# Decoder layer on one core: attention scores as two 64-column tiles in one run, root batches re-cut, mixing after the next queries' transposes

## The chip, the cores and the metric

One core of a Trainium2 chip runs the whole program in one launch. The time is device time in microseconds (us) for one execution. The engines are named as the profile names them: PE (matrix products; PEld is its weight load), DVE (VectorE), ACT (ScalarE), POOL (GpSimd) and SP (the queue that issues most transfers). All data is 32-bit floating point; each matrix product of the kernel appears in the trace as two matmul instructions.

## The reference

A pre-norm decoder layer over `x` of shape (16, 64, 512), in three residual steps:

```python
x = x + self_attention_over_batch(layernorm(x))
x = x + cross_attention(layernorm(x), ctx, mask, Wq, Wk, Wv, Wo, q_norm_w, k_norm_w)
x = x + mixture_of_experts(layernorm(x), gate_w, bias, Wg, Wu, Wd, Sg, Su, Sd)
```

The change lies in the cross attention. Each of the 16 batches has 64 query rows and 64 context rows, 32 query heads of 128, and 8 key/value heads, each shared by a group of 4 query heads:

```python
q = rmsnorm(q, q_norm_w)              # q = hidden @ Wq.T, root over the 128 of one head
k = rmsnorm(repeat(k, 4), k_norm_w)
scores = einsum('bhqd,bhkd->bhqk', q, k) / sqrt(128) + attention_mask
probs = softmax(scores)
out = einsum('bhqk,bhkd->bhqd', probs, v) ... @ Wo.T
```

The experts (16, the best 4 per token, plus a shared one) come after it and are not touched.

## The kernel before, in words

**Stages.** The 1024 tokens are 8 tiles of 128 rows; a tile holds two batches of 64. The batch attention, the keys and the values come first (to about 160 us), then the cross attention (about 165 to 745 us), then routing and experts. At 32-bit width the products with Wq and Wo are done by a seven-product scheme (`seven`, line 240) whose 14 matrix products are all recorded at line 254, with sums of the weights formed on POOL (`right_sums`, lines 235 to 238) and sums of the left operands (`left_sums`, lines 228 to 231).

**Steps of the cross attention.** `cross` (line 591) walks over pairs (g, u): g is one of 8 key/value heads, u one of 4 pairs of token tiles. For g from 0 to 5 a step does the following, in the text of the program:

- `softmaxed(g, u)` (line 490): for each of the two tiles, `normed_queries` (line 477) multiplies the raw queries by their roots on DVE (line 479), turns them on PE (line 482), and scales them by `q_norm_w` on the way out of PSUM on ACT (line 484) into `qt`. Then four products per tile form the scores (line 499). One product takes 128 columns of `qt` (two heads of 64 queries) as the stationary operand and 64 key columns as the moving one. DVE adds the mask (line 504), takes the maximum, subtracts it, ACT takes the exponential, DVE sums and normalises (lines 511 to 523).
- `queries(...)` (line 446): the Wq product for the step three places ahead, combined by DVE out of PSUM (lines 458 to 462), and the sums of squares on ACT (line 466).
- `projected(...)` (line 553): the Wo product of the step before, added into the running sums by DVE (lines 560 to 567).
- `attended(g, u, pr)` (line 526): turns the probabilities on PE (line 529), copies them out on ACT (line 533), mixes the values on PE (line 539), copies the result out on ACT (line 545) and forms the left sums on POOL (on DVE for g of 6 and 7).

For g of 6 and 7 the two heads alternate, and the steps also carry the layer norm, the routing and the table entries of the finished tiles.

**Roots.** `inverse_root` (line 440) takes a square root on ACT (line 442, each with a table load) and a reciprocal on DVE (line 443), for several tile pairs at once, whenever u is in `done`: after u = 0 and after u = 3 in every group but the last, so the second batch covers three tile pairs (24 roots per partition).

**Order.** The program's text is not the order on the engines: a scheduler places the instructions of each engine in a fixed order when the program is built, and semaphores enforce the data dependences. Each engine then works strictly through its own list. PSUM is used through rotating banks: 3 for the large products (`mm`), 2 for transposes (`tr`), 3 for scores, mixing and one of the seven products (`sc`).

In a regular step PE's list before the change is: probabilities turned, queries of the first tile turned, one Wq product, values mixed, scores of the first tile, queries of the second tile turned, two Wq products, scores of the second tile, the rest of Wq, all of Wo.

Of the kernel before, what the change touches and what calls it, by code (L numbers as in the profile page):

```python
# [25 lines left out]
AF = mybir.ActivationFunctionType  # L26
ALU = mybir.AluOpType
AX = mybir.AxisListType

P = 128  # L30
N, C, L = 16, 64, 512
NT = N * C // P
DC = L // P
KVH, GRP, HD = 8, 4, 128
# [8 lines left out]
SURE = 32  # L43
WB = 4
ROUND = float(3 << 22)


@with_exitstack
def decoder_layer(
# [25 lines left out]
    V, S, T, G = nc.vector, nc.scalar, nc.tensor, nc.gpsimd  # L75
# [17 lines left out]
    def tr_bank():  # L93
        return bank("tr", 2)

    def sc_bank():
        return bank("sc", 3)
# [6 lines left out]
    kT = [p.tile([P, KVH // 2, NT * P], F32, tag="kT", name="kT") for p in (kvp0, kvp)]  # L104
# [75 lines left out]
    qw_sb = const.tile([P, 1], F32, tag="qw", name="qw_sb")  # L180
# [52 lines left out]
    def right_sums(engine, t, w):  # L233
        b11, b12, b21, b22 = (w[:, 2 * k : 2 * k + 2, 256 * n : 256 * n + 256] for k in range(2) for n in range(2))
        engine.tensor_sub(t[:, 0], b12, b11)
        engine.tensor_sub(t[:, 1], b22, t[:, 0])  # L236
        engine.tensor_sub(t[:, 2], b21, t[:, 1])  # L237
        engine.tensor_sub(b12, b22, b12)
# [164 lines left out]
    for n0 in range(0, N, 4):  # L403
        for k in range(2):
            tp = tr_bank()
# [23 lines left out]
    q_raw, q_ss, q_rs = {}, {}, {}  # L429
# [16 lines left out]
    def queries(g, u):  # L446
        w = wq_tiles[g]
        if u == 0:
            q_ss[g] = small.tile([P, NT, GRP], F32, tag="qss", name="qss", bufs=2)
            if g > 0:  # L450
                right_sums(G, wq_t, w)
        raws = [work.tile([P, GRP, HD], F32, tag="qraw", name="qraw", bufs=8) for _ in range(2)]
        c1, c2 = (raw.rearrange("p (a h) d -> p a (h d)", a=2) for raw in raws)
        x, p7, p, r = seven(*xn_quarters(u), xn_sums[u], wq_t, w, sums_last=(g, u) == (0, 0))
        su = work.tile([P, 2, 256], F32, tag="su", name="su", bufs=1)
        u3 = work.tile([P, 256], F32, tag="u3", name="u3", bufs=1)
        S.copy(su[:, 0], x[:, 0])
        V.tensor_add(su[:, 1], x[:, 1], su[:, 0])
        V.tensor_add(u3, p7, su[:, 1])
        V.tensor_add(c1, p, su)  # L460
        V.tensor_add(c2, r, u3.unsqueeze(1).to_broadcast([P, 2, 256]))
        V.tensor_add(c1[:, 1], r[:, 1], c1[:, 1])
        for j, raw in enumerate(raws):
            for h in range(GRP):
                square = work.tile([P, HD], F32, tag="square", name="square", bufs=1)
                S.activation(square, raw[:, h, :], AF.Square, accum_out=q_ss[g][:, 2 * u + j, h : h + 1])  # L466
            q_raw[g, 2 * u + j] = raw

        done = (0, 1, 2, 3) if g == KVH - 1 else (0, 3)
        if u in done:  # L470
            first = max([k + 1 for k in done if k < u], default=0)
            span = 2 * (u + 1 - first)
            rs = inverse_root(q_ss[g][:, 2 * first : 2 * u + 2, :], [P, span, GRP], 1.0 / HD)
            for k in range(first, u + 1):
                q_rs[g, k] = rs[:, 2 * (k - first) : 2 * (k - first) + 2, :]

    def normed_queries(g, i):
        raw = q_raw.pop((g, i))
        V.tensor_mul(raw, raw, q_rs[g, i // 2][:, i % 2, :].unsqueeze(2).to_broadcast([P, GRP, HD]))  # L479
        tp = tr_bank()  # L480
        for j in range(GRP):
            T.transpose(tp[:, j * P : (j + 1) * P], raw[:, j, :], ident)  # L482
        qt = work.tile([P, 2, GRP, C], F32, tag="qt", name="qt", bufs=2)
        S.activation(  # L484
            qt.rearrange("p b h q -> p h b q"),
            tp.rearrange("p (h b q) -> p h b q", h=GRP, b=2), AF.Copy, scale=qw_sb,
        )
        return qt

    def softmaxed(g, u):  # L490
        sp = sc_bank()
        for j in range(2):
            i = 2 * u + j
            qt = normed_queries(g, i)
            for hp in range(2):
                for b in range(2):
                    k0 = i * P + b * C
                    at = ((j * 2 + hp) * 2 + b) * C
                    T.matmul(  # L499
                        sp[:, at : at + C], qt[:, b, 2 * hp : 2 * hp + 2, :],  # L500
                        kT[g // 4][:, g % 4, k0 : k0 + C], start=True, stop=True,
                    )
        pr = work.tile([P, 8, C], F32, tag="prob", name="prob")
        V.scalar_tensor_tensor(  # L504
            pr, sp.rearrange("p (a k) -> p a k", a=8), HD**-0.5,
            mask_sb.unsqueeze(1).to_broadcast([P, 8, C]), ALU.mult, ALU.add,
        )
        mx = small.tile([P, 8], F32, tag="mx", name="mx")
        sm = small.tile([P, 8], F32, tag="sm", name="sm")
        if g < KVH - 2:  # L510
            V.tensor_reduce(mx, pr, AX.X, ALU.max)
            V.tensor_sub(pr, pr, mx.unsqueeze(2).to_broadcast([P, 8, C]))
            S.activation(pr, pr, AF.Exp)
            V.tensor_reduce(sm, pr, AX.X, ALU.add)
        else:

            V.tensor_reduce(mx, pr, AX.X, ALU.max, negate=True)
            for a in range(8):
                S.activation(
                    pr[:, a, :], pr[:, a, :], AF.Exp, bias=mx[:, a : a + 1], accum_out=sm[:, a : a + 1]  # L520
                )
        V.reciprocal(sm, sm)
        V.tensor_mul(pr, pr, sm.unsqueeze(2).to_broadcast([P, 8, C]))
        return pr

    def attended(g, u, pr):
        tp = tr_bank()
        for a in range(4):
            T.transpose(
                tp[:, a * P : (a + 1) * P], pr[:, 2 * a : 2 * a + 2, :], ident  # L530
            )
        pt = work.tile([P, 2, 2 * P], F32, tag="pt", name="pt", bufs=1)
        S.copy(pt.rearrange("p j t -> p (j t)"), tp)
        at = work.tile([P, 2 * GRP, P], F32, tag="at", name="at", bufs=1)
        pv = [sc_bank() for _ in range(2)]
        for j in range(2):
            for b in range(2):
                rows = slice(b * C, (b + 1) * C)
                T.matmul(
                    pv[b][:, j * 256 : (j + 1) * 256],  # L540
                    v[g // 4][rows, 2 * u + j, g % 4 * HD : (g % 4 + 1) * HD], pt[rows, j, :],
                    start=True, stop=True,
                )
        for b in range(2):
            S.copy(at[:, :, b * C : (b + 1) * C], pv[b].rearrange("p (a q) -> p a q", a=2 * GRP))  # L545
        quarters = [at[:, 2 * k : 2 * k + 2, :] for k in range(4)]
        s = work.tile([P, 3, 2, P], F32, tag="sat", name="sat", bufs=1)
        left_sums(G if g < KVH - 2 else V, s, *quarters)
        return quarters, s
# [39 lines left out]
    late = []  # L589

    def cross(steps):
        for g, u in steps:
            if u == 1 and g + 2 < KVH:
                load_wq(g + 2)
            if u == 0 and g + 1 < KVH:
                load_wo(g + 1)
            pr = softmaxed(g, u)
            if g < KVH - 2:
                queries(*divmod(NT // 2 * g + u + 3, NT // 2))
            elif g == KVH - 2:  # L600
                queries(g + 1, u)
            if (g, u) == (KVH - 3, NT // 2 - 1):
                queries(g + 1, u)
            if late:
                projected(*late.pop())
            if (g, u) == (KVH - 1, NT // 2 - 1):
                shared_hidden(0, 0, mm_bank)
            late.append((g, u, *attended(g, u, pr)))
            if g == KVH - 2 and u > 0:
                summed(u - 1)  # L610
                normed_pair(u - 1)
                if u > 1:
                    entered(u - 2, 1)
            if g == KVH - 1 and u > 0:
                routed_pair(u - 1)
                entered(u - 1, 0)
            if (g, u) == (KVH - 2, 0):
                load_shared(0)
            if (g, u) == (KVH - 2, NT // 2 - 1):
                load_shared(1)  # L620
# [80 lines left out]
    def routed_pair(u):  # L701
# [64 lines left out]
        V.tensor_scalar(col, got, 1.0 / P, (P - 1) / (2.0 * P), ALU.mult, ALU.subtract)  # L766
        V.tensor_scalar(col, col, ROUND, ROUND, ALU.add, ALU.subtract)
        row = route.tile([P, 2 * TOPK], F32, tag="row", name="row", bufs=1)
# [335 lines left out]
```

## Time and profile before

| what | value |
|---|---|
| median of 3 runs | 1022.65 us (1020.56 to 1023.68) |
| profiled execution, its own time | 1023.92 us |
| its span, first to last instruction | 1022.1 us |
| mean granted clock of PE | 0.989 |
| PE busy | 975.9 us, 95% of the span |
| DVE, ACT, POOL busy | 527.0, 461.3, 329.1 us |
| scores on PE (line 499) | 512 matmuls, 69.7 us busy, 280 ns each |
| scaling of the turned queries on ACT (line 484) | 64 of 689 ns |
| roots times raw queries on DVE (line 479) | 64 of 1028 ns on average |

Busy time is the sum of the durations; matmuls overlap in the array, so the mean of 280 ns is longer than the distance from one matmul to the next. What a run of matmuls costs is read from the start times of a timeline. An average over the span hides the stages: PE is bound by its own work in the cross attention up to about 590 us, has waits between about 600 and 745 us, and works for the experts after that.

### The profile page before, as it was taken

To read this page: it belongs to the slowest core of one execution; us is meant where nothing else is said; L and a number is where in the kernel's file an instruction comes from. 1 tells how busy PE (TensorE), PEld (TensorE's weight loads), DVE (VectorE), ACT (ScalarE), POOL (GpSimd) and SP (SyncE) were. 2 spreads that over 40 slices of the span, in tenths; PEclk is the share of its full clock that TensorE was granted. 3 is DMA by queue.
4 is the path that set the end of the run, shared out by engine and by line. 5 is a ranking of instruction groups with operands and counts; after the bars stand their busy time and mean duration, and the time that the engine had idled before them with its cause. 6 is when DMAs were issued, how large, how long until landed. Compare 5 with 4: busy or idle time off the path is not lost. (4 is left out here: it accounts for less than half of the span.)

```text
span 1022.1 us, 13777 instructions
## 1 busy us (share of the span) xinstructions
PE 975.9 (95%) x4568; PEld 683.7 (67%) x4568; DVE 527.0 (52%) x1116; ACT 461.3 (45%) x1283; POOL 329.1 (32%) x356
## 2 busy tenths in 40 slices
PE   8999998999999999998999999979999999999994
PEld 3456555788888888887888887767664454544542
DVE  4565757674845756648457567667476111111110
ACT  2366662664454545545545475555530222222221
POOL 2132111421612516236235142032133444454433
PEclk9999999999999999999999999989899999999998
DMA  9120014200201102012010010000023966655663
GB/s 240 61 93 21 11 42 114 83 1 1 83 1 43 42 1 83 1 52 83 1 46 39 9 75 1 21 22 22 21 53 126 390 155 154 144 97 138 179 182 76
DMA packets 28956, 76.80 MB, mean 75 GB/s; under 512 B 4625, under 2 KB 9025, under 8 KB 26833
## 3 DMA queue, kind: packets, MB, share of 16 engines
q1 hardware_dynamic: 18160, 52.96, 15.4%
q0 software_dynamic: 10432, 22.66, 10.9%
q8 instruction: 38, 0.62, 0.2%
q14 instruction: 38, 0.30, 0.1%
q10 hardware_dynamic: 288, 0.26, 0.1%
HBM read 102.31 MB, written 14.97 MB: 115 GB/s over the span
## 5 line engine op out<-in xcount | busy, mean ns | idle before, releaser
L967 PE MATMUL sc<-w,xt 128*128 128x512 f32 x288 | 130.3, 593 | 2.3 <-DMA w<-in_wu_dram 2.2
L466 ACT ACTIVATE square<-qraw 128x128 f32<-128x128 f32 x256 | 79.1, 309 | 60.0 <-DVE qraw L460 29.2
L967 PEld LDWEIGHTS sc<-w,xt 128*128 128x128 f32 x288 | 51.8, 190 | 54.1 <-issue 52.2
L228 POOL TENSOR_TENSOR sat<-at 128x256 f32<-128x256 f32 x24 | 19.7, 821 | 210.0 <-ACT at L545 209.9
L972 DVE TENSOR_TENSOR z<-sc,z 128x256 f32<-128x256 f32 x36 | 15.3, 424 | 124.5 <-ACT z L971 120.0
L499 PEld LDWEIGHTS sc<-kT,qt 128*128 128x128 f32 x512 | 61.8, 191 | 19.1 <-ACT qt L484 11.0
L254 PE MATMUL mm<-wq_t,xns 128*128 128x256 f32 x256 | 70.7, 385 | 2.9 <-POOL wq_t L236 1.8
L254 PE MATMUL mm<-wo_sb,at 128*128 128x256 f32 x256 | 68.6, 394 | 5.0 <-ACT at L545 5.0
L254 PE MATMUL mm<-wq_sb,xnT 128*128 128x256 f32 x256 | 70.4, 381 | 0.0
L995 POOL DMA_INDIRECT out_dram<-y,idx x36 | 57.3, 1592 | 40.0 <-DMA out_dram<-y,idx 35.4
L499 PE MATMUL sc<-kT,qt 128*128 128x64 f32 x512 | 69.7, 280 | 0.3
L987 PE MATMUL mm<-w,zt 128*128 128x512 f32 x144 | 68.0, 594 | 1.6 <-DVE zt L980 1.0
L254 PE MATMUL mm<-wo_t,sat 128*128 128x256 f32 x256 | 67.5, 384 | 0.5 <-DVE sat L229 0.5
L479 DVE TENSOR_TENSOR qraw<-qraw,rs 128x512 f32<-128x512 f32 x64 | 63.5, 1028 | 0.5
L949 POOL DMA_INDIRECT xg<-rows_d,idx x40 | 39.6, 990 | 72.2 <-PE tr L978 49.5
L793 POOL DMA_INDIRECT table_d<-entry_sb,at_slot x24 | 25.6, 1068 | 114.7 <-DVE at_slot L760 108.3
L971 ACT ACTIVATE z<-sc 128x256 f32<-128x256 f32 x36 | 13.8, 383 | 107.0 <-PE sc L967 98.3
L504 DVE SCALAR_TENSOR_TENSOR prob<-sc,mask_sb 128x512 f32<-128x512 f32 x32 | 22.0, 688 | 77.2 <-PE sc L499 77.2
L254 PEld LDWEIGHTS mm<-wo_sb,at 128*128 128x128 f32 x256 | 49.6, 196 | 13.6 <-ACT at L545 6.8
L254 PEld LDWEIGHTS mm<-wo_t,sat 128*128 128x128 f32 x256 | 48.5, 193 | 7.1 <-POOL wo_t L237 0.6
L254 PEld LDWEIGHTS mm<-wq_t,xns 128*128 128x128 f32 x256 | 46.7, 190 | 8.7 <-POOL wq_t L236 2.0
L484 ACT ACTIVATE qt<-tr,qw_sb 128x512 f32<-128x512 f32 x64 | 43.8, 689 | 18.3 <-PE tr L482 18.3
(283 smaller groups left out, 2056.7 us busy)
## 6 DMA issues: line engine op xcount, KB each, us to landing
w<-in_wg_dram SPq DMA_DIRECT2D x40, 512.0 KB
w<-in_wu_dram SPq DMA_DIRECT2D x40, 512.0 KB
w<-in_wd_dram SPq DMA_DIRECT2D x40, 512.0 KB
wq_sb<-in_wq_dram SPq DMA_DIRECT2D x8, 1024.0 KB
wo_sb<-in_wo_dram SPq DMA_DIRECT2D x8, 1024.0 KB
xs<-in_x_dram SPq DMA_DIRECT2D x8, 256.0 KB
wv_sb<-in_wv_dram SPq DMA_DIRECT2D x2, 1024.0 KB
ct<-in_ctxt_dram SPq DMA_DIRECT2D x8, 256.0 KB
```

The source lines that it names most:

```text
L228: engine.tensor_add(s[:, 0], a21, a22)
L254: T.matmul(dst, left[:, k, :], right[:, k, :], start=k == 0, stop=k == 1)
L466: S.activation(square, raw[:, h, :], AF.Square, accum_out=q_ss[g][:, 2 * u + j, h : h + 1])
L479: V.tensor_mul(raw, raw, q_rs[g, i // 2][:, i % 2, :].unsqueeze(2).to_broadcast([P, GRP, HD]))
L484: S.activation(qt.rearrange("p b h q -> p h b q"), tp.rearrange("p (h b q) -> p h b q", h=GRP, b=2), AF.Copy, scale=qw_sb,)
L499: T.matmul(sp[:, at : at + C], qt[:, b, 2 * hp : 2 * hp + 2, :], kT[g // 4][:, g % 4, k0 : k0 + C], start=True, stop=True,)
L504: V.scalar_tensor_tensor(pr, sp.rearrange("p (a k) -> p a k", a=8), HD**-0.5, mask_sb.unsqueeze(1).to_broadcast([P, 8, C]), ALU.mult, ALU.add,
L793: G.indirect_dma_start(tables_d[q], bass.IndirectOffsetOnAxis(at_slots[u][:, q : q + 1], axis=0), entry_sb[:, 2 * u + j, k, :], None,)
L949: G.indirect_dma_start(xg, None, rows_d, bass.IndirectOffsetOnAxis(idx[:, b : b + 1], axis=0))
L967: T.matmul(hp, xt[:, d, :], w1_tiles[buffer(j)][:, :, d, :], start=(d == 0), stop=(d == DC - 1))
L987: T.matmul(op, zt[:, c, :], w2_tiles[buffer(j)][:, c, :], start=(c == 0), stop=(c == FI // P - 1))
L995: G.indirect_dma_start(out, bass.IndirectOffsetOnAxis(idx[:, b : b + 1], axis=0), y, None, bounds_check=NT * P - 1, oob_is_err=False, comp ...
```

## The change

Four things change in the cross attention.

1. **Scores.** Each score product takes one head (64 columns of `qt`) as the stationary operand. The two heads of a pair write to partitions 0 to 63 and 64 to 127 of the same PSUM bank: two column tiles of the array. There are 16 products of 64x64 per step in place of 8 of 128x64, all in one run behind the queries of both tiles.
2. **Queries first.** `step_queries` turns and scales both tiles ahead of the mixing of the step before. For g up to 5 the second tile is scaled by DVE and not by ACT, and a DVE operation on 8 elements per partition multiplies the first column of the first tile's `qt` by the comparison of the second tile's with a huge number, that is by 1. This makes all scores wait for both tiles.
3. **Roots.** `done` is (1, 3), and (0, 1, 3) for g = 0: batches of two tile pairs, 16 roots per partition. The roots of the next step are multiplied by a comparison of the masked scores with the huge number (by 1 again), on DVE, so the scaling of the next step's queries waits for the masked scores of this one.
4. **Mixing.** `attended` is split: `turned_rows` stays, the mixing of step k is recorded after the query transposes of step k + 1, except at the end of a walk and for g of 6 and 7.

```diff
-        done = (0, 1, 2, 3) if g == KVH - 1 else (0, 3)
+        done = (0, 1, 2, 3) if g == KVH - 1 else (0, 1, 3) if g == 0 else (1, 3)
...
-    def normed_queries(g, i):
+    def normed_queries(g, i, on_vector):
...
+        turned = tp.rearrange("p (h b q) -> p h b q", h=GRP, b=2)
+        if on_vector:
+            V.tensor_scalar(qt.rearrange("p b h q -> p h b q"), turned, qw_sb, None, ALU.mult)
+        else:
+            S.activation(qt.rearrange("p b h q -> p h b q"), turned, AF.Copy, scale=qw_sb)
         return qt

-    def softmaxed(g, u):
+    def step_queries(g, u):
+        qts = [normed_queries(g, 2 * u + j, j == 1 and g < KVH - 2) for j in range(2)]
+        if g < KVH - 2:
+            first, second = (qt[:, :, :, 0:1] for qt in qts)
+            V.scalar_tensor_tensor(first, second, HIGHEST, first, ALU.is_le, ALU.mult)
+        return qts
+
+    def softmaxed(g, u, qts):
         sp = sc_bank()
...
+        for hp in range(2):
+            for b in range(2):
+                for j, qt in enumerate(qts):
...
-                    T.matmul(
-                        sp[:, at : at + C], qt[:, b, 2 * hp : 2 * hp + 2, :],
-                        kT[g // 4][:, g % 4, k0 : k0 + C], start=True, stop=True,
-                    )
+                    for h in range(2):
+                        T.matmul(
+                            sp[h * C : (h + 1) * C, at : at + C], qt[:, b, 2 * hp + h, :],
+                            kT[g // 4][:, g % 4, k0 : k0 + C], start=True, stop=True,
+                        )
...
+        after = divmod(NT // 2 * g + u + 1, NT // 2)
+        if after[0] < KVH - 2:
+            rs = q_rs[after]
+            V.scalar_tensor_tensor(
+                rs, pr[:, 0:1, 0:1].to_broadcast([P, 2, GRP]), HIGHEST, rs, ALU.is_le, ALU.mult
+            )
...
-            pr = softmaxed(g, u)
+            qts = step_queries(g, u)
+            if mixing:
+                late.append((*mixing[:2], *attended(*mixing)))
+                mixing = None
+            pr = softmaxed(g, u, qts)
...
-            late.append((g, u, *attended(g, u, pr)))
+            pt = turned_rows(pr)
+            if g < KVH - 2 and (g, u) != steps[-1]:
+                mixing = (g, u, pt)
+            else:
+                late.append((g, u, *attended(g, u, pt)))
```

In a regular step PE's list after the change is: probabilities turned, queries of the first tile turned, one Wq product, queries of the second tile turned, values mixed, all 16 score products, the rest of Wq, all of Wo.

More of the change, by code (lines that the diff above doesn't have):

```diff
@@ L45 @@
 ROUND = float(3 << 22)
+HIGHEST = 3.0e38
 @with_exitstack
@@ L483, in normed_queries @@
         qt = work.tile([P, 2, GRP, C], F32, tag="qt", name="qt", bufs=2)
-        S.activation(
-            qt.rearrange("p b h q -> p h b q"),
-            tp.rearrange("p (h b q) -> p h b q", h=GRP, b=2), AF.Copy, scale=qw_sb,
-        )
-        return qt
-    def softmaxed(g, u):
-        sp = sc_bank()
[L492 to L497, printed above, removed]
-                    at = ((j * 2 + hp) * 2 + b) * C
-                    T.matmul(
-                        sp[:, at : at + C], qt[:, b, 2 * hp : 2 * hp + 2, :],
-                        kT[g // 4][:, g % 4, k0 : k0 + C], start=True, stop=True,
-                    )
+        turned = tp.rearrange("p (h b q) -> p h b q", h=GRP, b=2)
[3 more added lines that the diff above has]
+            S.activation(qt.rearrange("p b h q -> p h b q"), turned, AF.Copy, scale=qw_sb)
+        return qt
+    def step_queries(g, u):
[5 more added lines that the diff above has]
+    def softmaxed(g, u, qts):
+        sp = sc_bank()
+        for hp in range(2):
+            for b in range(2):
+                for j, qt in enumerate(qts):
+                    k0 = (2 * u + j) * P + b * C
+                    at = ((j * 2 + hp) * 2 + b) * C
+                    for h in range(2):
[3 more added lines that the diff above has]
+                        )
         pr = work.tile([P, 8, C], F32, tag="prob", name="prob")
@@ L524, in softmaxed, with turned_rows @@
         return pr
-    def attended(g, u, pr):
+    def turned_rows(pr):
         tp = tr_bank()
@@ L533, in attended @@
         S.copy(pt.rearrange("p j t -> p (j t)"), tp)
+        return pt
+    def attended(g, u, pt):
         at = work.tile([P, 2 * GRP, P], F32, tag="at", name="at", bufs=1)
@@ L596, in cross @@
                 load_wo(g + 1)
-            pr = softmaxed(g, u)
+            qts = step_queries(g, u)
+            if mixing:
+                late.append((*mixing[:2], *attended(*mixing)))
+                mixing = None
+            pr = softmaxed(g, u, qts)
             if g < KVH - 2:
```

## The prediction

> **What bounds the kernel now.** I read the page first: which engine is full, and at what clock. Lines of parts 1 and 2:
>
> ```profile
> PE 975.9 (95%) x4568; PEld 683.7 (67%) x4568; DVE 527.0 (52%) x1116; ACT 461.3 (45%) x1283; POOL 329.1 (32%) x356
> PEclk9999999999999999999999999989899999999998
> ```
>
> PE is full and its clock is granted, so a change counts if it takes PE time away or makes PE wait. Next the waits of PE from 198 to 590 us, the steps with g up to 5:
>
> ```profile
> PE tr L482 <- DVE qraw L479: 3.9, 6, 2.4
> PE mm L254 <- POOL wq_t L236: 1.8, 1, 1.8
> ```
>
> Only 5.7 us of 392 are waits; the rest is PE's own list. So I priced one step in PE's timeline (start, busy us, line):
>
> ```profile
> 417.80 0.60 PE L529 MATMUL tr<-ident,prob 128*128 128x128 f32 x4
> 418.24 0.60 PE L482 MATMUL tr<-ident,qraw 128*128 128x128 f32 x4
> 418.68 0.60 PE L254 MATMUL mm<-wq_sb,xnT 128*128 128x256 f32 x2
> 419.21 1.14 PE L539 MATMUL sc<-pt,v 64*128 64x256 f32 x8
> 420.28 1.10 PE L499 MATMUL sc<-kT,qt 128*128 128x64 f32 x8
> 421.22 0.61 PE L482 MATMUL tr<-ident,qraw 128*128 128x128 f32 x4
> 421.66 0.60 PE L254 MATMUL mm<-wq_sb,xnT 128*128 128x256 f32 x2
> 422.10 0.59 PE L254 MATMUL mm<-wq_t,xns 128*128 128x256 f32 x2
> 422.61 1.10 PE L499 MATMUL sc<-kT,qt 128*128 128x64 f32 x8
> 423.55 0.65 PE L254 MATMUL mm<-wq_t,xns 128*128 128x256 f32 x2
> ...
> 434.39 0.27 PE L529 MATMUL tr<-ident,prob 128*128 128x128 f32 x1
> ```
>
> From start to start the step is 434.39 - 417.80 = 16.59 us. Each run of scores takes 0.94 (421.22 - 420.28, 423.55 - 422.61), two per step 1.88. The price of two column tiles can be read in the batch attention, line 358, whose products have the new shape but for the moving columns. The windows of line 358, then of line 499 (length, PE busy with matmuls in flight, the same for weight loads):
>
> ```profile
> 63.91:64.02 0.11, 0.11 (x8) 0.11 (x4) 1.00 0.54 225
> 403.98:404.09 0.11, 0.11 (x4) 0.11 (x3) 1.00 0.00 0
> ```
>
> Both matmuls last 273 to 275 ns; line 358 has twice as many in flight, so its two tiles run side by side, two starts per 0.11 us. Last the stalls outside the regular step, and two prices on DVE:
>
> ```profile
> 471.00 0.55 PE L482 MATMUL tr<-ident,qraw 128*128 128x128 f32 x3 [2.42 <-DVE qraw L479]
> L504 DVE SCALAR_TENSOR_TENSOR prob<-sc,mask_sb 128x512 f32<-128x512 f32 x32 | 22.0, 688 | 77.2 <-PE sc L499 77.2
> L522 DVE RECIPROCAL sm<-sm 128x8 f32<-128x8 f32 x32 | 6.2, 194 | 5.2 <-ACT prob L519 4.7
> ```
>
> **The change, part by part.** t0 is the start of a step's probability transposes, S the start of its scores.
>
> *Scores.* Before, 16 matmuls per step start every 0.112 us although they stream only 64 columns (256 columns take 0.216, so 64 take 0.054): the load of 128 weight columns sets the pace. A load of 64 columns lasts 137 ns (line 358), one of 128 lasts 192 (line 499), so 64 columns are 0.055. After, 32 matmuls form 16 rounds of two. The best round is 0.055 (load and stream of 64 columns overlap), the worst is that of line 358, 0.109, which streams 128 columns. I take 0.057, because in line 358's first round the next pair of loads starts 55 ns after the first pair, so two tiles' loads don't queue behind each other. With 0.11 to fill, 0.11 + 16 x 0.057 = 1.02 against 1.88: -0.86 per step (bounds -0.9 and 0). In the 24 steps with g up to 5 PE is the bound: -20.6.
>
> The Trainium skill, TensorE: Matmul & The Clock Gate, section Back-to-back issue gap, gives a floor of about 25 ns per matmul at 1 to 64 columns. If weight loads paid it as well, an estimate for 64 instructions is 1.6 us per step, and the sum would be 0.58 x 24 = 14 us worse; line 358 at 27 ns per instruction doesn't exclude it, its pairs 7 ns apart speak against it.
>
> *One run in place of two.* The second entry goes: 422.61 - 422.10 = 0.51 and 424.04 - 423.55 = 0.49 for pairs that else take 0.43, about 0.1 per step. -2.4 (bounds -3.4, 0). The other entries stay (values at 419.21 come 0.1 late, and the scores behind them 0.2 after their last pair).
>
> *Second tile scaled on DVE, and the gate.* The scores wait for both. DVE starts 0.20 us after the matmul run it waits for (423.55, line 504 at 423.75); 688 ns is the nearest row for a 128x512 read out of PSUM, and a dependent operation follows 0.72 later (424.47). The 8-element gate is like line 522's 0.19, plus 0.06 to PE. From the end of the second tile's transposes that is 0.20 + 0.72 + 0.19 + 0.06 = 1.17. Cover: the mixing, 420.28 - 419.21 = 1.07. So +0.1 per step, +2.5 in all (bounds 0 and 12, the latter if DVE comes 0.4 later because a reciprocal waiting for ACT and the last addition of Wo stand ahead of it). On ACT 0.69 per step goes, which nobody waits for. Queued behind the scaling on DVE are the mask and the combinations out of PSUM, which wait for PE anyway.
>
> *Roots and gate of the roots.* The count of batches is unchanged but for one more at g = 0 (two table loads of 1.28 on ACT, beside PE). Batch u = 3 is first needed one step later than before. Steps with the late batch show up as 17.05 in place of 16.59 (starting at 267, 334, 401, 537), the one at 467.56 as 19.54 with the 2.42 wait above: 4 x 0.46 + 2.95 = 4.8, which goes. The next step's queries are multiplied on DVE (line 479, 0.60 apart when undisturbed) right after the mask. They stand ahead of the operations that free PSUM banks. Worked through: mask at S + 1.2, two multiplications and the softmax pieces, last Wq bank freed at S + 8.3, needed by Wo's last two products at S + 11.0. POOL's left sums (4 x 0.72 from about S + 1.4) collide with them; line 479 under POOL sums was 1.67 apart at 403 to 408 us. I allow 1.0 to 2.0 for it: banks are still in time. The squares on ACT then end up to 1 us later, and with a table load and root behind them the copy of the probabilities (line 533) is late by about 0.1 to 0.3 in 12 steps: +1.2 (bounds 0, 6).
>
> *Order.* In the first step PE idles from 199.3 to 201.2 for POOL's wq_t; the new list does transposes, mixing and scores there: -1.5 (bounds -1.9, 0). At the switch to g = 4, DVE's list has a clearing of `taken` (line 697), which waits for the last mixing of the first heads, ahead of the scaling: scaling and gate then start after the mixing and not beside it, +1.3 once. Lists of POOL and SP keep their order.
>
> *The 8 steps with g of 6 and 7.* Scores save 8 x 0.86 = 6.9, but ACT still scales both tiles, with two copies of the mixed values (0.5 each) ahead of the second: PE has 0.44 + 0.98 of work from the end of the mixing, ACT is ready about 2.0 after it. I take 0.35 per step, +2.8, and +1.3 for one step in which a table load now precedes the copy of the probabilities. -2.8 (bounds -7, +3).
>
> Sum: -20.6 - 2.4 + 2.5 - 4.8 + 1.2 - 1.5 + 1.3 - 2.8 = -27.1. The experts' stage just moves forward. Against the profiled execution's own 1023.92 (span 1022.1 and 1.8 around it, 1.3 above the median of the runs) that is 996.8; against the median 995.6. I say 997.
>
> **The rivals.**
>
> 1. *The rounds stay near 0.109*, because the array pays per round, the loads of the two tiles take turns, or instructions are issued no faster than in line 358 (4 per 0.109, 27 ns each, the densest run that a row shows). For it: no row shows a round under 0.109. Against: line 358's loads start in pairs 7 ns apart, the next pair 55 ns on. The scores then cost 1.85, so the -20.6 and most of the last 8 steps' gain go, and the rest stands: 997 + 20 = 1017 at the worst, 1012 if the rounds are half way. The floor of the Trainium skill's page, if it held for loads too, would give 1011 (997 + 14), an estimate.
>
> 2. *Slower: DVE comes late to the scaling in every step.* Place: DVE's list between the last addition of Wo and the scaling. In the step shown above line 567 ran only at 419.57, 1.77 after t0, behind a reciprocal that waited for ACT. The gain per step is about 0.96; if the scaling starts over 1.0 later than I say in all 24 steps, the change loses. At 1.3 more: 997 + 24 x 1.3 = 1028. Against: the scaling is due only at t0 + 1.95, and the multiplications that stood there before are gone.
> 3. *The tiles don't run side by side* because both write one PSUM bank: 32 x 0.112 = 3.6 per step, 32 x 1.7 = 54 more than before, 1070. Line 358 writes one bank too and runs in pairs.
>
> **How the numbers follow.** Forecast 0.68 (988 to 1006, from the bounds of DVE's chain, the roots and the last 8 steps), rivals 1: 0.20, 2: 0.10, 3: 0.02. The range goes from the forecast's lower end into rival 1: 987 to 1016; it leaves out 2, 3 and a little of 1. No change is within 0.3%, 3 us, about what a measurement can tell. Faster: the forecast and rival 1, less 0.03 for the part of 1 that reaches 1020: 0.85; same: that 0.03 and 0.01 of rival 2; slower: the rest of rivals 2 and 3, 0.11.
>
> **What would show it.** In PE's timeline a regular step of about 15.7; scores as one run of 32 with about 1.0 to the next start; windows of that run with about 8 matmuls in flight per 0.11. No wait of PE on the multiplied queries; a small wait of PE on DVE's gate ahead of the scores, about 0.1. The step at 467 us without its 2.4. If rounds are at 0.11 the run takes 1.85 and rival 1 holds; if PE's waits name DVE's `qt` with over 0.5 a step, rival 2 is at work. A miss elsewhere would be collisions with POOL at a group's start, seen as waits of PE on ACT's copy of the probabilities.

## The result, and the profile after

The changed kernel takes 1009.0 us (median of 4 runs, 1008.3 to 1013.4; the profiled execution 1009.14, its span 1007.4). The longest of the four runs had a granted clock of 0.983, the others 0.989 or 0.990. The kernel before took 1022.1 beside it. The ratio is 0.988, with a 95% interval of 0.985 to 0.991: 13 us less, 1.2%. The prediction was 997, 25.6 under the median of before, with a range of 987 to 1016. The time lies inside the range, but half of the gain is missing.

PE is as full as before, at the same clock. Parts 1 and 2 of the page after:

```profile
PE 956.2 (95%) x5080; PEld 662.8 (66%) x5080; DVE 552.4 (55%) x1188; ACT 445.0 (44%) x1260; POOL 336.3 (33%) x356
PEclk9999999999999999999999999998999999999997
```

A regular step in PE's timeline after the change (start, busy us, line; what a row costs is the distance to the next start):

```profile
410.70 0.60 PE L546 MATMUL tr<-ident,prob 128*128 128x128 f32 x4
411.14 0.60 PE L483 MATMUL tr<-ident,qraw 128*128 128x128 f32 x4
411.57 0.60 PE L255 MATMUL mm<-wq_sb,xnT 128*128 128x256 f32 x2
412.01 0.62 PE L483 MATMUL tr<-ident,qraw 128*128 128x128 f32 x4
412.56 1.13 PE L559 MATMUL sc<-pt,v 64*128 64x256 f32 x8
413.76 1.15 PE L509 MATMUL sc<-kT,qt 128*64 128x64 f32 x32
414.84 0.70 PE L255 MATMUL mm<-wq_sb,xnT 128*128 128x256 f32 x2
...
426.60 0.60 PE L546 MATMUL tr<-ident,prob 128*128 128x128 f32 x4
```

The run of scores takes 414.84 - 413.76 = 1.08, against twice 0.94 before. The step is 15.90 long, against 16.59: 0.69 less. Between the mixing and the scores 1.20 pass, where 1.07 passed before: the scores now wait 0.13 for the gate. The windows of line 509 answer those of lines 358 and 499:

```profile
413.90:414.01 0.11, 0.11 (x8) 0.11 (x8) 1.00 0.00 0
```

Eight matmuls, as many as for line 358, and eight weight loads, twice as many, are in flight in 0.11 us. This window begins 0.14 us into the run; in the middle of it, from 414.20 to 414.31, it is twelve matmuls and eight loads. In the records of single instructions the matmuls start in pairs, 6 to 7 ns apart, a new pair every 58 to 59 ns. So the two column tiles do run side by side, at about the pace that was forecast (0.057).

What is missing shows in the waits of PE from 198 to 590 us (waited for: us in total, times, longest). Before, the same view named 5.7 us; now it names about 10:

```profile
PE sc L509 <- DVE qt L497: 5.6, 7, 1.4
PE tr L483 <- ACT pt L550: 2.6, 5, 1.4
PE mm L255 <- POOL wq_t L237: 1.5, 1, 1.5
```

Line 497 is the gate of the queries, line 550 the copy of the turned probabilities. Most of these waits lie in the steps just after a group's start; the others are in the first step (1.5 on `wq_t`), in the step ahead of the switch to g = 4 (0.5 on the gate) and in the 24th (1.4 on the gate). Just after a group's start the change has steps of 17.01 where its regular step is 15.90 (starts at 264, 329, 394, 525), and one of 18.46 at 459. The timeline of all engines around the step at 394:

```profile
387.90 1.27 POOL L236 TENSOR_TENSOR wq_t<-wq_sb 128x512 f32<-128x512 f32 x1 [2.00 <-PE mm L255]
387.96 1.75 DVE L540 TENSOR_TENSOR prob<-prob,sm 128x512 f32<-128x512 f32 x1
...
393.33 1.28 ACT L443 ACT_TABLE_LOAD   x1
394.62 0.31 ACT L443 ACTIVATE rs<-qss,eps_sb 128x16 f32<-128x16 f32 x1
394.84 0.57 ACT L550 COPY pt<-tr 128x512 f32<-128x512 f32 x1
395.46 0.66 PE L483 MATMUL tr<-ident,qraw 128*128 128x128 f32 x4 [0.29 <-ACT pt L550]
396.51 1.27 POOL L239 TENSOR_TENSOR wo_sb<-wo_sb 128x512 f32<-128x512 f32 x1
397.01 0.80 DVE L497 SCALAR_TENSOR_TENSOR qt<-qt 128x8 f32<-128x8 f32 x1
397.86 1.15 PE L509 MATMUL sc<-kT,qt 128*64 128x64 f32 x32 [0.68 <-DVE qt L497]
```

Two things happen. POOL's sums of Wq's weights run beside DVE from 387.9 on: the operation of line 540 takes 1.75 in place of 0.67, the raw queries come late, and so do ACT's squares. The table load and the root then stand ahead of the copy of the probabilities, and PE waits for that copy. Three us later the gate, an operation on 8 elements per partition that lasts 0.17 elsewhere, takes 0.80: it began while POOL's sum of line 239 ran, and ends when that ends (396.51 + 1.27 = 397.78). The longest such step answers the row at 471 of before:

```profile
461.92 0.66 PE L483 MATMUL tr<-ident,qraw 128*128 128x128 f32 x4 [1.39 <-ACT pt L550]
464.68 1.15 PE L509 MATMUL sc<-kT,qt 128*64 128x64 f32 x32 [1.03 <-DVE qt L497]
```

The mean of DVE's multiplications by the roots fell from 1028 to 757 ns. Before, PE waited for them six times, 3.9 us in all; now the view names no such wait, and PE gets nothing from the rest of the fall:

```profile
L480 DVE TENSOR_TENSOR qraw<-qraw,rs 128x512 f32<-128x512 f32 x64 | 48.2, 757 | 0.2
```

Where the 14.8 us of the span come from, by the starts of the steps: to the third turning of the probabilities -1.5, the 20 steps from there -10.9 (336.5 to 325.6), the next step +0.6, the last eight -3.5, from there to the end +0.5.

### The profile page after: what moved, and what is told of

The parts are those of the page before. It is cut to its first block, busy times and chain, and to the rows that moved or that the text cites. A ratio compares the mean times of both kernels' runs of the same rounds, so it can differ in the third digit from the quotient of the medians.

```text
span 1007.4 us, 14841 instructions
## 1 busy us (share of the span) xinstructions
PE 956.2 (95%) x5080; PEld 662.8 (66%) x5080; DVE 552.4 (55%) x1188; ACT 445.0 (44%) x1260; POOL 336.3 (33%) x356
## 5 line engine op out<-in xcount | busy, mean ns | idle before, releaser
L229 POOL TENSOR_TENSOR sat<-at 128x256 f32<-128x256 f32 x24 | 17.5, 728 | 202.2 <-ACT at L565 202.2
L255 PE MATMUL mm<-wq_sb,xnT 128*128 128x256 f32 x256 | 72.5, 389 | 0.0
L255 PE MATMUL mm<-wq_t,xns 128*128 128x256 f32 x256 | 66.2, 381 | 2.6 <-POOL wq_t L237 1.5
L823 POOL DMA_INDIRECT table_d<-entry_sb,at_slot x24 | 25.6, 1065 | 111.6 <-DVE at_slot L790 105.2
L1017 PEld LDWEIGHTS mm<-w,zt 128*128 128x128 f32 x144 | 27.1, 190 | 35.3 <-issue 32.1
L565 ACT COPY at<-sc 128x512 f32<-128x512 f32 x64 | 34.3, 588 | 35.3 <-PE sc L559 35.0
L480 DVE TENSOR_TENSOR qraw<-qraw,rs 128x512 f32<-128x512 f32 x64 | 48.2, 757 | 0.2
L255 PEld LDWEIGHTS mm<-wq_sb,xnT 128*128 128x128 f32 x256 | 44.3, 190 | 5.7 <-DVE su L459 0.3
L467 ACT ACTIVATION_READ_ACCUMULATOR square<-qraw 128x1 f32 x256 | 47.8, 187 | 0.0
```

What stands on the lines that cost most here:

```text
L229: engine.tensor_add(s[:, 0], a21, a22)
L255: T.matmul(dst, left[:, k, :], right[:, k, :], start=k == 0, stop=k == 1)
L823: G.indirect_dma_start(tables_d[q], bass.IndirectOffsetOnAxis(at_slots[u][:, q : q + 1], axis=0), entry_sb[:, 2 * u + j, k, :], None,)
L1017: T.matmul(op, zt[:, c, :], w2_tiles[buffer(j)][:, c, :], start=(c == 0), stop=(c == FI // P - 1))
```

## The experiments

Theory: the shorter rounds pay as forecast, the regular step loses only the gate's 0.13, and the missing half is lost at the groups' starts, to POOL's sums: through the gate and through the root ahead of the copy. Rivals: something other than PE's list sets the regular step; the batches of roots themselves are at fault; the gate's delay is covered.

The table gives, from the profiled execution of each kernel, the regular step, the steps just after a group's start, the 20 steps from the third to the twenty-third turning of the probabilities, and then the medians and the ratios to the kernel before on the same chip.

| kernel | regular step | group's start | 20 steps | median us | ratio (95%) |
|---|---|---|---|---|---|
| before | 16.59 | 17.05 (19.54) | 336.5 | 1022.1 | 1 |
| the change | 15.90 | 17.01 (18.46) | 325.6 | 1009.0 | 0.988 (0.985 to 0.991) |
| wide | 16.60 | 16.60 (17.77) | 333.7 | 1026.0 | 1.004 (1.002 to 1.006) |
| tiles_in_turn | 16.65 | 17.76 (17.82) | 339.1 | 1030.5 | 1.007 (1.005 to 1.008) |
| sums_once | 15.90 | 15.90 (17.13) | 319.8 | 1014.3 | 0.991 (0.989 to 0.994) |
| gate_psum | 15.77 | 16.25 (17.35) | 320.8 | 1004.7 | 0.981 (0.978 to 0.984) |
| no_gate | 15.77 | 16.25 (17.35) | 319.4 | 1003.1 | 0.982 (0.979 to 0.984) |
| roots_shift | 15.90 | 15.90 or 17.01 (16.15) | 322.8 | 1005.5 | 0.985 (0.982 to 0.988) |
| roots_only | 16.58 | 16.58 (16.95) | 332.0 | 1016.0 | 0.993 (0.991 to 0.995) |
| columns_only | 16.04 | 16.38, then 16.61 (20.11) | 328.8 | 1010.4 | 0.987 (0.986 to 0.989) |
| roots_columns | 16.04 | 16.04 (17.50) | 322.7 | 1003.7 | 0.981 (0.979 to 0.983) |
| best | 15.77 | 15.77 (15.83) | 317.3 | 999.7 | 0.978 (0.976 to 0.981) |
| best_no_gate | 15.77 | 15.77 (15.77) | 317.4 | 1000.2 | 0.978 (0.976 to 0.980) |

In brackets the step at the switch to g = 4 (at 467.56 before, 459.06 after).

**The column tiles undone (wide).**

```diff
-                    for h in range(2):
-                        T.matmul(
-                            sp[h * C : (h + 1) * C, at : at + C], qt[:, b, 2 * hp + h, :],
+                    T.matmul(
+                        sp[:, at : at + C], qt[:, b, 2 * hp : 2 * hp + 2, :],
```

> The changed kernel with the score products as 128x64 again (16 per step in one run, no column tiles); all else as in the change. Theory (PE's own list bounds the steps, and the shorter rounds are the whole gain): the run of scores goes from 1.08 to about 1.88 us, the 24 steps with g up to 5 lose 0.80 each, 19.2, and the last 8 between 0 and 6.4: 1028 to 1035, so above the kernel before, because the other parts then cost more than they bring. Rival (something else than PE's list sets the step after the change, and half of the shorter rounds is lost in waits): less than 0.5 per step comes back, under 1021.

It took 1026.0, 2 under the theory's range and 5 over the rival's. The profiled execution, whose steps the table has, was the quickest of seven (1023.1). The run of scores costs 1.83 (404.95 to 406.78) where 1.88 was expected, and the pair behind it comes 0.05 earlier than in the change, so the regular step is longer by 0.70 and not by 0.80:

```profile
404.95 2.00 PE L508 MATMUL sc<-kT,qt 128*128 128x64 f32 x16
406.78 0.65 PE L255 MATMUL mm<-wq_sb,xnT 128*128 128x256 f32 x2
```

So PE's list sets the step, and without the column tiles the rest of the change leaves the kernel no faster than before, by 0.4% slower. What was not expected: the steps at a group's start are regular here, 16.60. With longer scores they are shorter than in the change (17.01). The run with the shifted roots shows below how narrow that is.

**The two tiles one after the other (tiles_in_turn).**

```diff
-        for hp in range(2):
-            for b in range(2):
-                for j, qt in enumerate(qts):
+        for h in range(2):
+            for hp in range(2):
+                for b in range(2):
+                    for j, qt in enumerate(qts):
```

> The changed kernel with the 16 products of a step in another order: first all 8 that write partitions 0 to 63, then all 8 that write 64 to 127. Theory (the gain is that products of two column tiles run side by side, so neighbours must be of different tiles): the run takes 1.7 to 1.9 again, 24 x 0.7 more: 1024 to 1028. Rival (the pace is that of loading 64 columns, whichever tile): the run stays at 1.08, 1008 to 1011.

```profile
423.95 1.90 PE L508 MATMUL sc<-kT,qt 128*64 128x64 f32 x32
425.78 0.70 PE L255 MATMUL mm<-wq_sb,xnT 128*128 128x256 f32 x2
```

The same 32 matmuls of the same shape take 1.83, and the time is 1030.5, 2.5 above the theory's range, which counted 24 steps only: the last eight take 5.2 more than in the change as well. The steps at a group's start are 1.11 longer than the regular one, as in the change, but here it is all the gate's (1.29 at 405.96). The records show one matmul every 58 ns in place of two. So within one tile a load and a matmul of 64 columns come every 58 ns, and the second tile ran beside the first only where its instructions stood next in the list.

**POOL's sums left out (sums_once).**

```diff
-            if g > 0:
-                right_sums(G, wq_t, w)
...
+            if 0 < g < KVH - 1:
+                wo_sums[g] = wo_sums[0]
+            else:
...
```

> The changed kernel, leaving out work: POOL forms the sums of the weights of Wq for g = 0 only and those of Wo for g = 0 and g = 7 only; the other groups use the sums of g = 0, so the output is another one. Theory (the extra time of the steps at a group's start comes from these POOL operations, which hold up DVE's gate, its multiplications and with them ACT's squares and root): these steps fall to 15.9, which gives 4 x 1.11 + 2.56 = 7.0, the wait of 1.5 in the first step goes too, and up to 2 in the last 8 steps: 998 to 1002. Rival (the extra time comes from the batch of roots itself, its table load and reciprocal): the steps stay above 16.5, 1006 to 1009.

The steps decide for the theory in four places of five: 15.90 just after a group's start, with the same batches of roots and table loads in place. At the switch to g = 4 the step is 17.13, so 1.23 of its 2.56 stays without these sums. There DVE's list has the routing's constants ahead of the mask of the step before, and they wait 2.74 for POOL's `part_i` (DVE idle up to 444.52); by the rows the squares, the root and the copy come late behind them, which is read from the trace and was not tested by a run of its own. The 20 steps fall by 5.9 (325.64 to 319.75). The median went up all the same, to 1014.3, a miss of the expectation in time: from the last turning of the probabilities to the end this kernel takes 1011.4 - 715.3 = 296.1 us and the change 285.6, with 36 more matmuls on PE (5116 against 5080), which fits experts that get other tokens from the other output. Only its cross attention can be compared.

**The gate on PSUM, and no gate (gate_psum, no_gate).**

```diff
-            first, second = (qt[:, :, :, 0:1] for qt in qts)
-            V.scalar_tensor_tensor(first, second, HIGHEST, first, ALU.is_le, ALU.mult)
+            first = qts[0][:, :, :, 0:1].rearrange("p b h q -> p (b h) q")
+            V.scalar_tensor_tensor(
+                first, tps[1][:, 0:8].unsqueeze(2), HIGHEST, first, ALU.is_le, ALU.mult
+            )
```

> The changed kernel with one edit: the 8-element gate of the queries reads the second tile's turned queries in PSUM and no longer their scaled copy in SBUF. Theory (the gate, with two operands in SBUF, is held until POOL's running operation ends): the gate takes about 0.17 in the steps at a group's start too, in place of 0.80 to 1.15, which gives 4 x 0.63 + 1.0 = 3.5, and the step no longer waits for the end of the second scaling: up to 0.1 x 24 more. 1003 to 1006. Rival (DVE or ACT is late there anyway, the gate's length is covered): 1008 to 1010.

It took 1004.7, as the theory said. The rows of DVE and POOL at the group's start, with the gate again in the middle of POOL's sum:

```profile
392.66 1.27 POOL L239 TENSOR_TENSOR wo_sb<-wo_sb 128x512 f32<-128x512 f32 x1
392.96 0.16 DVE L497 SCALAR_TENSOR_TENSOR qt<-tr,qt 128x8 f32<-128x8 f32 x1
393.25 1.15 PE L511 MATMUL sc<-kT,qt 128*64 128x64 f32 x32
```

With one operand in PSUM the gate takes 0.16 under the same operation of POOL under which it took 0.80 with both in SBUF. The regular step loses its 0.13 too. What stays at a group's start is 0.48, the copy behind the root.

The Trainium skill, SBUF — State Buffer, section Who interferes with whom, says that a DVE instruction with two SBUF inputs and a POOL instruction that reads SBUF need the same read port, that the first to start has it for its whole length, and that a DVE instruction with one SBUF input is not concerned (outside its two-port modes). The three durations of the gate (0.80, 0.16, and 0.17 where POOL rests) agree with that.

Leaving the gate out altogether hardly moves PE's list (two products of scores change place in the first step, and two of scores with one of Wq in the step ahead of the switch):

```diff
-        if g < KVH - 2:
-            first, second = (qt[:, :, :, 0:1] for qt in qts)
-            V.scalar_tensor_tensor(first, second, HIGHEST, first, ALU.is_le, ALU.mult)
```

> The changed kernel without the 8-element gate of the queries; the order of PE's instructions stays but for two products in the first step. Theory (the gate costs 0.13 in each step, more under POOL's sums, and buys nothing that the order of the instructions doesn't give): as with the gate on PSUM, steps of 15.77 and 16.25 at a group's start, 1003 to 1006. Rival (the scores then stall in the run on the second tile, whose scaling ends late): steps of 15.9 or more, 1008 to 1010.

1003.1 and the same steps as with the gate on PSUM, but for the one ahead of the switch to g = 4: 16.24 in place of 17.65. DVE's list there now has the mask ahead of the routing's constants and no longer behind them. In the regular steps the order of the list alone does what the gate was put in for.

**The roots in other steps (roots_shift).** The change takes roots in the steps (g, 2) and (g, 0); POOL's sums lie at the end of (g, 0) and behind it. Here the batches are (g, 1) with (g, 2) and (g, 3) with (g + 1, 0):

```diff
+        start = (g, u) if (g, u) in done else (g, 1) if u in (1, 2) else (g, 3) if u == 3 else (g - 1, 3)
...
-        if u in done:
+        if (g, u) in done or (g, u) != start:
```

> The changed kernel with the batches of roots cut as (g,1) with (g,2) and (g,3) with (g+1,0), so that no root is taken in the step (g,0) in which POOL forms its sums; the first pair of all alone, and single pairs from g = 6's last on. Theory (at a group's start the table load and the root stand ahead of the copy of the probabilities because the squares are late): the 0.48 of that goes in four steps and 1 or so in the one at 459, the gate's wait stays: these steps about 16.5, 1005 to 1007. Rival (the squares alone, or DVE's order, hold the copy up): the steps stay at 17.0, 1008 to 1010.

PE no longer waits for the copy of the probabilities anywhere from 215 to 535 us, and the median is 1005.5, inside the theory's range. But single steps are not what it gave: some are 15.90, others still 17.01. The rows of DVE and POOL for the starts of g = 1 and g = 3 show why:

```profile
266.30 0.18 DVE L500 SCALAR_TENSOR_TENSOR qt<-qt 128x8 f32<-128x8 f32 x1
266.30 1.31 POOL L239 TENSOR_TENSOR wo_sb<-wo_sb 128x512 f32<-128x512 f32 x1
...
394.60 1.29 DVE L500 SCALAR_TENSOR_TENSOR qt<-qt 128x8 f32<-128x8 f32 x1
394.60 1.26 POOL L239 TENSOR_TENSOR wo_sb<-wo_sb 128x512 f32<-128x512 f32 x1
```

The gate and the sum start at the same hundredth. At g = 1 the gate's record is 6 ns ahead, and POOL's sum takes 0.04 more; at g = 3 POOL's is 1 ns ahead, and the gate waits for its whole length. At g = 5 (523.68) the gate's record is 2 ns ahead and it waits all the same (1.30), so the records do not settle what decides such a tie. This is the gate alone: 1.11 per step. It also explains wide and tiles_in_turn, in which PE does not wait for the copy at these starts: the former's gate met the same sum at the same moment (both at 404.72) and won, the latter's lost.

**Parts of the change on the kernel before (roots_only, columns_only, roots_columns).**

```diff
-        done = (0, 1, 2, 3) if g == KVH - 1 else (0, 3)
+        done = (0, 1, 2, 3) if g == KVH - 1 else (0, 1, 3) if g == 0 else (1, 3)
```

> The kernel before with the batches of roots as in the change, (0, 1, 3) and then (1, 3), and nothing else of it. Theory 1 (as in the prediction: the late batch was the cause of the longer steps): four steps fall from 17.05 to 16.59 and the one of 19.54 to about 16.6, so 4.8 less than before: 1017. Theory 2 (the squares are late because POOL's sums slow DVE at a group's start, and whatever comes behind them is late whichever pair it is for): the root's table load now holds up the copy of the turned probabilities, the steps stay at 17 or so, 1020 to 1023.

The roots alone bring what the prediction had put down for them: every step 16.58, the one at the switch 16.95, 4.5 over the 20 steps, 1016.0. Theory 1 holds, in the old order. Next the column tiles alone, the lines of the first experiment's diff the other way round:

> The kernel before with the score products as two column tiles (two runs of 16 matmuls per step in place of two of 8 products with 128 columns), nothing else of the change. Theory (the shorter rounds need neither one run nor the new order): each run falls from 0.94 to 0.11 + 8 x 0.0585 = 0.58 or a little more, 0.70 per regular step as in the change, 24 x 0.70 = 17, and 0 to 5 in the last 8 steps; the steps with late roots keep their extra: 1000 to 1006. Rival (two short runs pay their entry twice, or the second tile's scaling on ACT is then late): 0.3 to 0.5 per step, 1010 to 1015.

They bring 0.55 per step, under the 0.70 that the theory gave: each run costs 0.61 in place of 0.94 (the forecast was 0.58), and the products behind each run start 0.05 later than before. They also bring out a stall: with the shorter step PE waits for the copy of the probabilities just after the groups' starts (0.5 at the longest). So 1010.4, the rival's figure. The rows of the two runs:

```profile
414.31 0.69 PE L500 MATMUL sc<-kT,qt 128*64 128x64 f32 x16
414.92 0.66 PE L482 MATMUL tr<-ident,qraw 128*128 128x128 f32 x4
...
416.37 0.69 PE L500 MATMUL sc<-kT,qt 128*64 128x64 f32 x16
416.99 0.70 PE L254 MATMUL mm<-wq_t,xns 128*128 128x256 f32 x2
```

Then both edits together:

> The kernel before with the column tiles and the changed batches of roots, but with its own order: each tile's queries turned, scaled on ACT and scored in a run of their own, no gates, mixing where it was. Theory (the new order and the gates bring nothing and cost the gate's waits): 7.5 from the batches and 17 to 20 from the column tiles, 996 to 1000, so faster than the change. Rival (shorter steps bring the root's table load under POOL's sums in this order as well): the steps at a group's start take 16.3 and more, 1002 to 1007.

It takes 1003.7 (996 to 1000 was expected, with 0.70 per step in place of 0.55), with an interval apart from that of the change: these two edits, a few lines, beat the whole change by about 5 us. The time is in the rival's range, but the rival's longer steps at a group's start are not there (16.04, and 17.50 at the switch alone). The old order scales both tiles on ACT and has no gate. POOL's sums slow DVE here too: three multiplications by the roots take 4.52 us (line 479 at 392.80), and PE does not wait for them; its only listed wait from 215 to 535 us is 1.4 at the switch.

**The causes taken away together (best, best_no_gate).**

```diff
-    V.memset(taken[:, 0, :], 0.0)
+    G.memset(taken[:, 0, :], 0.0)
```

with the gate on PSUM (or none) and the shifted batches.

> The changed kernel with the gate on the second tile's PSUM, the batches of roots shifted as in the run with (g,1), (g,2) and (g,3), (g+1,0), and the clearing of taken on POOL in place of DVE. Theory (the causes add up): steps of 15.77 throughout, 4 x 0.48 at the groups' starts and 2 to 3 about the switch to g = 4 less than with the gate on PSUM alone: 999 to 1002, faster than every kernel so far. Rival (a collision with POOL's sums moves to another operation): a wait of 0.5 to 1 at the groups' starts, 1002 to 1005.

> The same with the gate of the queries left out altogether. Theory: as with the gate on PSUM, 999 to 1002. Rival (as for the kernel without the gate alone): 1 to 3 more.

999.7 and 1000.2: every step at a group's start is regular, 15.77 (15.83 at the switch in the former). The two don't differ. Both are about 1% faster than the change (0.978 with intervals up to 0.981, against 0.985 to 0.991). From 215 to 535 us PE waits once in the former, in the step before the switch to g = 4 (17.06 long), where DVE's list has the routing's constants, which wait for POOL, ahead of the mask:

```profile
PE mm L255 <- DVE qraw L466: 0.5, 1, 0.5
```

Two parts were not measured alone, so their shares are not shown: the clearing of `taken` on POOL, and the gate of the roots, which stands in every kernel with the new order.

## Where the prediction was right, and where it lost half

The forecast was 25.6 us less, and 13.1 were measured. The pace of the column tiles was right; what went wrong is the sum around it. The step that failed most is the one on the roots: the extra of the steps at a group's start was to go (-4.8), with only 1.2 for a late copy in its place. The runs show these steps 2.2 dearer than before, because in them the copy waits for a root and the gate, priced at 0.19, for POOL's sum. The other misses are smaller; each has its line here:

| term of the sum | predicted | measured |
|---|---|---|
| scores, 24 steps | -20.6 | -19.3 (1.88 to 1.08 each) |
| one run in place of two | -2.4 | -0.5 (0.02 each) |
| second scaling and gate, regular steps | +2.5 | +3.1 (0.13 each) |
| late roots | -4.8 | +2.2 (extras of 7.0 in place of 4.8) |
| roots ahead of the copy, spread over 12 steps | +1.2 | 0 in regular steps; it is in the row above |
| first steps | -1.5 | +0.6 |
| clearing of `taken` | +1.3 | +0.7 |
| the 24th step (at 558) | 0 | +1.3 |
| last eight steps | -2.8 | -3.5 |
| from there to the end | 0 | +0.5 |
| sum | -27.1 | -14.9, against -14.8 of the profiled times |

**The scores** were priced nearly right: 0.0585 per round where 0.057 was taken, and one run of 1.08 where 1.02 was given, 1.3 over 24 steps. Rivals 1 and 3 fall: the run with the tiles in turn shows one matmul per 58 ns, the change two. The Trainium skill, TensorE: Matmul & The Clock Gate, section Back-to-back issue gap, gives a floor of about 25 ns per matmul; had it held for weight loads as well, the run would have taken 1.6, an estimate. The 64 instructions take 1.08, 17 ns each, so the loads don't pay it; and the second matmul of each pair starts 6 to 7 ns after the first, so the floor holds at most as a mean over a pair (29 ns). Two prices of these rivals do not follow from their own terms: with 1.85 for the scores most of the last eight steps' gain goes too, so rival 1 reaches about 1020 and not 1017 (the part on the chances uses 1020), and rival 3's 54 on top of the median before is 1077 and not 1070.

**One run in place of two** failed as a term against the kernel before. "The second entry goes" was right: the pairs about the second run no longer take 0.51 and 0.49. But the pair behind the one run now takes 0.53 (414.84 to 415.37) where others take 0.43, and that the prediction did not count: 0.02 per step is left. Against two runs of short tiles the order with one run is worth 0.27 (16.04 with two runs, 15.77 with one and no gate), which only the runs could show.

**The gate** in a regular step was forecast at 0.1 and cost 0.13. What failed is the price of the gate itself: "The 8-element gate is like line 522's 0.19". Line 522 has one operand. The gate has two in SBUF, and the prediction's own rows of line 479 under POOL's sums (1.67 apart) were those of an operation of that kind; the step applied them to the multiplications and not to the gate. At a group's start it took 0.80 to 1.15, and the gate on PSUM gives that back.

**The late roots** were the largest miss: 7.0 in their row, 5.8 with the 1.2 of the next row, of 12.2 in all. The step that failed is "4 x 0.46 + 2.95 = 4.8, which goes", together with the 0.1 to 0.3 by which the copy of the probabilities was to be late. In the old order it is right: the batches alone brought 4.5. In the new order the wait for late roots is replaced by two others in the very steps in which POOL forms its sums. The prediction did name the place in its last paragraph (collisions with POOL at a group's start, seen as waits on the copy of the probabilities), but priced it at 1.2 as if it were spread over 12 steps. By the runs the 1.11 of four steps is made of the root ahead of the copy, 0.48 (it goes with the shifted batches), and the gate under line 239, the rest. Of the 2.56 at the switch, 1.23 is there without POOL's sums as well (sums_once), behind the routing's constants on DVE.

**The first steps.** That "the new list does transposes, mixing and scores there" was a misreading: the list puts two products with the new sums ahead of the turning, and the wait of 1.5 on `wq_t` stays. The stages ahead of the cross attention, which the change does not touch, ended 1.1 later in this execution than in that of before (in that of no_gate 0.4 earlier), so 1.1 of the 2.1 missed here is not the change's.

**The 24th step** was not seen. There a batch of roots ends only at 558.3, 0.2 into the step; four multiplications that wait for it stand ahead of the gate on DVE, and PE waits 1.37 for the gate. That is rival 2 in one step out of 24. In the other steps DVE came in time. With the shifted batches the step is 21.9 in place of 23.3, and the one before it 0.65 longer.

**The last eight steps** came out 0.7 better than forecast; why was not looked into.

## What to carry to other kernels

When a step gets shorter, look at the few irregular steps first: the regular one was predicted within 0.2 us (about 15.7 against 15.90), and about half of the loss lay in five steps of twenty. A small operation on the critical path costs what its operands cost: with two operands in SBUF the gate waited for the sum that POOL ran beside it (0.80 to 1.29), and with one in PSUM it didn't (0.16). Before adding a gate to hold an order, try the order without it. And when parts of a change are separable, measure each alone: here two edits of a few lines were worth more than the whole.

## What the runs showed of the hardware that was not expected

- An operation of DVE on 8 elements per partition, both operands in SBUF, takes 0.17 us alone and 1.29 us if a sum of POOL on 128x512 elements began just before it; if it begins first, POOL loses 0.04. With both starting within 0.01 us it went either way, and moved a step by 1.11.
- Two column tiles of 64 reach one matmul per 29 ns with a weight load for each, if they alternate; the same instructions in blocks of 8 products (16 matmuls) per tile reach one per 58 ns.
- A shorter run of scores made some steps longer (there the gate fell behind POOL's sum and the copy behind a root): 17.01 against 16.60 with scores 0.75 longer.
